# A graph network kernel on one core: loads, checks and scalings moved to other engines and slots

## The chip, the cores and the metric

The kernel runs on one core of one Trainium2 chip. The core has TensorE (matmuls; PE in the profile, PEld for its weight loads), VectorE (DVE), ScalarE (ACT), GpSimd (POOL) and SyncE (SP), each with a queue of its own that it works off in order. Sixteen DMA engines carry the transfers that SP, ACT and POOL issue. The metric is the device time of one execution in microseconds, as the median of several runs.

## What is computed

There are 16 graphs (B) of 1024 nodes (N) with 256 features (D). Each graph goes through two layers, and each layer ends with an addition and a norm over the features.

```python
# layer 0; adj holds 0 and 1 here, so only a0 counts
e0    = leaky(einsum('bid,bjd->bij', h * a0[:, 0], h))     # slope 0.2
alpha = sigmoid(where(adj == 1, e0, -huge))                # codes 2 to 4 use a1 to a3
x     = layernorm(x + einsum('bij,bjd->bid', alpha, h) + bias)
# layer 1
Hh = x @ W;  s = Hh @ a_src;  d = Hh @ a_dst
e  = where(adj != 0, exp(-leaky(s[:, None] + d[None, :])), 0)
x  = layernorm(x + elu((e @ Hh) / rowsum(e)))
```

Both norms are (x - mean) / sqrt(variance + 1e-5). The adjacency is symmetric and holds only 0 and 1; the kernel counts this while it runs, and a flag at the end decides whether a general version (`general_pass`) has to do the work again. With these inputs it does not.

## The kernel before

A graph passes through three stages, and TensorE goes through them one after the other. Nothing is scheduled by a tool inside `one_kind_pass`: the order of every engine's queue is the order in which the Python code emits the instructions (`manual_schedule`).

**Strips.** The score matrix is symmetric, so only the upper triangle is computed, in 8 strips of 128 rows (`strip(b, jt)`, L184 to L208). A strip has one or two pieces of up to 512 columns. For each piece TensorE multiplies x transposed (`xTs`) with x transposed and scaled by a0 (`xas`) into one of three PSUM banks (`ps_e`); ScalarE makes two tanh of it (`tb` at L206, `low` at L207, since a sigmoid is a tanh); VectorE takes their maximum (L208). `finish` (L214) adds one and multiplies by the adjacency, and POOL adds to the diagonal block (L224). The lower triangle is the mirror: for graph 0 TensorE transposes it (`mirror`, L252 and L253), for the others VectorE transposes blocks of 32 (`dump`, L230), SP writes them to DRAM (L234), `gather` (L238) reads them back and `mask` (L244) applies the adjacency. There are four `tb` buffers, so strip 4 and later wait until an earlier strip has been written out.

**First sum.** `sum0(b, t)` (L287 to L306) multiplies alpha with x for 128 rows, 8 tiles a graph. VectorE evicts each tile (L302) and takes mean and variance (`stats`, L264 and L265); after tiles 3 and 7 POOL works out one over the standard deviation (`rstd`, L267 to L280, six small operations). `scale0` then normalises a tile in place on VectorE (L283): x1.

**Second layer.** x1 has to be transposed for the projection: `save_x1` (L320) writes half a graph to DRAM, `fetch_x1` (`load_blocks`, L110, eight transfers) reads it back in blocks of 32, `turn_x1` (L331) transposes the blocks on VectorE. `project` (L343, and L351 to L353 on ScalarE) makes H and the two logits and stands between the strips of the next graph; `spread_p` (L362) spreads one logit along the rows. The second sum is `sum1` (L382) with `weights` (L375) as its factor; `elu` (L397 to L403) evicts a tile with three small operations on VectorE and a Relu and an Exp on ScalarE; `add` (L408, L409 and `stats`) finishes it on VectorE; the scaling of the second norm (`scale1`, L283, on VectorE) and the store (L432) come during the first sum of the graph two later.

So beside TensorE's stages of graph b, VectorE and ScalarE work on graphs b, b - 1 and b - 2. In the loop over b, `prev` is b - 1 and `done` is b - 2.

**Start and end.** x of graph 0 is transposed on TensorE (L179); x of the later graphs is loaded in blocks (`load_blocks`) and transposed on VectorE (`turn_x`, L169, and L170 on ScalarE). For graph 1 this load is issued by ScalarE's queue, for the others by SP's. `make_Wx` (L155 and L156) multiplies W with a, ahead of graph 0's first strip. `check_adj` (L116, ScalarE, 128x2048, four a graph, in the slots of tiles 4 to 7 of the first sum) counts the entries that are neither 0 nor 1. For graph 0 the strips 4 to 7 lie between the tiles of the first sum. For the last graph the scalings of the second norm are done on ScalarE (`scale1_act`, L425), with `center` (L412 to L420), which has POOL work out one over the deviation and minus the mean over the deviation.

Tiles of one tag share buffers: `a_bc` shares with p, graph 1's `xT` with y, and the check's `junk` with the products of `make_Wx`.

Of the kernel before, what the change touches and what calls it, by code (L numbers as in the profile page):

```python
# [9 lines left out]
F32 = mybir.dt.float32  # L10
# [3 lines left out]
AF = mybir.ActivationFunctionType  # L14
# [4 lines left out]
P = 128  # L19
# [10 lines left out]
def one_kind_pass(  # L30
# [70 lines left out]
                    continue  # L101
                nc.gpsimd.dma_start(adjs[b][v], rows[v])

    def load_blocks(dst, src, n0, n, queue=nc.sync):


        v = src[ds(n0, n), :].rearrange("(nb nn) (c q dd) -> q c nn nb dd", nn=SQ, c=ND, dd=SQ)
        for c in range(ND):
            for q in range(P // SQ):
                queue.dma_start(  # L110
                    dst[ts(q, SQ), c, ds(n0, n)].rearrange("p (nb dd) -> p nb dd", dd=SQ), v[q, c]
                )

# [28 lines left out]
    nc.gpsimd.memset(power, -0.5)  # L142
    bias_bc = const.tile([P, D], F32, tag="bias", name="bias_bc")
    nc.sync.dma_start(bias_bc, bias.partition_broadcast(P))
    a_bc = one.tile([P, 2 * D], F32, tag="p", name="a_bc")
    nc.sync.dma_start(a_bc, a[0].partition_broadcast(P))
    Wx = const.tile([P, ND, D + 2], F32, tag="Wx", name="Wx")
    nc.sync.dma_start(Wx[:, :, 2:], W.rearrange("(c p) o -> p c o", p=P))
# [130 lines left out]
        nc.gpsimd.tensor_tensor(r, r, n, ALU.mult)  # L279
        return r  # L280

    def scale(y, mv, r):
        nc.vector.tensor_scalar(y, y, mv[:, 0:1], r, ALU.subtract, ALU.mult)  # L283

    x1s, mv0s, r0s = {}, {}, {}

    def sum0(b, t):  # L287
        if t == 0:
            x1s[b] = two.tile([P, NT, D], F32, tag="x1", name=f"x1_{b}")
            mv0s[b] = small.tile([P, NT, 2], F32, tag="mv0", name=f"mv0_{b}")  # L290
            r0s[b] = {}
        acc = ps_acc.tile([P, D], F32, tag="acc", name=f"acc0_{b}_{t}")
        for jt in range(NT):
            nc.tensor.matmul(  # L294
                acc,
                lhsT=als[b][:, jt, ts(t, P)],
                rhs=xs[b][:, jt, :],
                start=(jt == 0),
                stop=(jt == NT - 1),
            )  # L300
        y = x1s[b][:, t, :]
        nc.vector.scalar_tensor_tensor(y, acc, 0.5, bias_bc, ALU.mult, ALU.add)  # L302
        stats(y, mv0s[b][:, t, :], f"0_{b}_{t}")
        if t % HT == HT - 1:
            g = t // HT
            r0s[b][g] = rstd(mv0s[b][:, ts(g, HT), :], f"0_{b}_{g}")  # L306

    def scale0(b, t):
        scale(x1s[b][:, t, :], mv0s[b][:, t, :], r0s[b][t // HT][:, t % HT : t % HT + 1])


    x1Ts, Hs, pqs, p_bcs, es = {}, {}, {}, {}, {}
# [16 lines left out]
    def turn_x1(b, g):  # L329
        v = x1Ts[b][:, :, ts(g, HALF)]  # L330
        nc.vector.transpose(v, v)  # L331
# [44 lines left out]
            es[b][:, m, :], p_bcs[b], pqs[b][:, m, 1:2], adjs[b][:, m, :], ALU.mult, ALU.min  # L376
        )

    hs, ys, mv1s, r1s, rms = {}, {}, {}, {}, {}

    def sum1(b, t, acc, m):
        nc.tensor.matmul(  # L382
# [29 lines left out]
    def center(b, t0, n):  # L412

        mv = mv1s[b][:, ds(t0, n), :]
        r = rstd(mv, f"1_{b}_{t0}")
        mr = small.tile([P, NT], F32, tag="mr", name=f"mr_{b}_{t0}")[:, 0:n]
        nc.gpsimd.tensor_tensor(mr, mv[:, :, 0], r, ALU.mult)
        nc.gpsimd.tensor_scalar(mr, mr, -1.0, None, ALU.mult)
        for t in range(n):
            rms[b, t0 + t] = r[:, t : t + 1], mr[:, t : t + 1]  # L420

    def scale1_act(b, t):
        y = ys[b][:, t, :]
        r, mr = rms[b, t]
        nc.scalar.activation(y, y, AF.Identity, bias=mr, scale=r)  # L425

    def scale1(b, t):
        scale(ys[b][:, t, :], mv1s[b][:, t, :], r1s[b][:, t : t + 1])

    def store(b, t0, n):  # L430
        rows = out[b].rearrange("(t p) d -> p t d", p=P)
# [7 lines left out]
    for g in range(2):  # L439
        for c in range(ND):  # L440
            transpose_x(0, g, c)
    make_Wx()
    strip(0, 0)
    for jt in range(HT):
        if jt < HT - 1:
            strip(0, jt + 1)
        finish(0, jt, 0, HALF)
        mirror(0, jt)
    load_x(1)
    new_xT(1)  # L450
    load_blocks(xTs[1], x[1], 0, N, nc.scalar)
    for t in range(NT):
        sum0(0, t)
        if t < HT:
            finish(0, t, HALF, N)
            strip(0, t + HT)
        if 1 <= t <= HT:
            finish(0, t + HT - 1)
            if t < HT:
                mirror(0, t + HT - 1)  # L460
        if t in (4, 5):
            scale0(0, 2 * t - 8)
            scale0(0, 2 * t - 7)
        if t == 5:
            save_x1(0, 0)
            fetch_x1(0, 0)
        if t in (5, 6):
            turn_x(1, t - 5)
        if t >= NT - CHECKS:
            check_adj(0, t - NT + CHECKS)  # L470

    for b in range(1, B):
        prev, done = b - 1, b - 2
        last = b == B - 1

        projects = [[jt] for jt in range(NT)]
        if prev == 0:

            projects = [[], [], [], [0, 1], [2, 3], [], [4, 5], [6, 7]]
        for jt in range(NT):  # L480
            strip(b, jt)
            if prev == 0 and jt in (1, 2):
                scale0(0, 2 * jt + 2)
                scale0(0, 2 * jt + 3)
            if prev == 0 and jt == 2:
                save_x1(0, 1)
                fetch_x1(0, 1)
            if prev == 0 and jt in (2, 5):
                turn_x1(0, (jt - 2) // 3)
            finish(b, jt)  # L490
            if jt < NT - 1:
                dump(b, jt)
            if jt >= 1:
                gather(b, jt - 1)
            for t in projects[jt]:
                project(prev, t)
            if jt >= 5:
                mask(b, jt - 5)
# [24 lines left out]
        if not last:  # L523
            load_adj(b + 1)


        for t in range(NT):
            acc = acc1(prev, t, ps_acc, "acc")
            for m in range(NT):
                sum1(prev, t, acc, m)  # L530
            if last and t == 6:
                turn_x1(b, 1)
            if last and t == 7:
                weights(b, 0)
                weights(b, 1)
            elu(prev, t, acc)
            if t >= 1:
                add(prev, t - 1)
            if t == 0:
                fetch_x1(b, 0)  # L540
            if t in (1, 2):
                scale0(b, 2 * t + 2)
                scale0(b, 2 * t + 3)
            if t == 2:
                save_x1(b, 1)
            if t == 4:
# [12 lines left out]


    last, done = B - 1, B - 2
    first = [acc1(last, t, ps_e, "e") for t in range(3)]
    for m in range(NT):
        if m >= 2:
            weights(last, m)
        if m == 3:
            add(done, NT - 1)
            center(done, 0, NT)
        for t in range(3):
            sum1(last, t, first[t], m)  # L570
    check_pq(last)
    for t in range(NT):
        if t < 3:
            acc = first[t]
        else:
            acc = acc1(last, t, ps_acc, "acc")
            for m in range(NT):
                sum1(last, t, acc, m)
        elu(last, t, acc)
        if t in (3, 6):  # L580
            center(last, t - 3, 3)
        add(last, t)
        if t == 6:
            center(last, 6, 1)
        for q in range(2 * t - 6, 2 * t - 4) if 3 <= t < 7 else []:
            scale1_act(done, q)
            if q in (3, 7):
                store(done, q - 3, HT)
        if t == 6:
            for q in range(3):  # L590
                scale1_act(last, q)
            store(last, 0, 3)
    for q in range(3, 7):
        scale1_act(last, q)
        if q == 5:
            store(last, 3, 3)
    center(last, 7, 1)
    scale1_act(last, 7)
    store(last, 6, 2)


# [389 lines left out]
```

## Time and profile before

| | us |
|---|---|
| median of 3 runs (lowest, highest) | 1329.43 (1328.62, 1329.67) |
| the profiled execution: time | 1330.3 |
| its span, first to last instruction | 1328.4 |
| TensorE busy | 1280.3 (96%) |
| VectorE busy | 1019.5 (77%) |
| ScalarE busy | 546.5 (41%) |
| POOL busy | 243.4 (18%) |
| one graph in the middle | 80.7 |
| mean granted TensorE clock | 0.992 |

The profile is of one execution, whose time stands beside its span. Times in it count from the span's start. A line of the timeline gives start, length, engine, code line, operation, written and read tile, shape and count; in brackets stand the idle time before it and what ended that. A wait is put down to what came last. Ends of matmuls are modelled, so neighbouring ones overlap by some 0.2 us. ACTq and SPq are the issue of transfers by that engine's queue.

### The profile page before, as it was taken

The page shows a single profiled execution, that of the slowest core. Times are in us where ns is not written, and L with a number is a line of the kernel's source. Part 1 is how long each engine was busy: PE and PEld are TensorE (multiplying, and loading weights), DVE is VectorE, ACT ScalarE, POOL GpSimd, SP SyncE. Part 2 cuts the span into 40 slices and gives each one's busy share as a digit, 9 for nine tenths or more (in the row PEclk, how much of TensorE's full clock was granted, in tenths as well). Part 3 has the DMA queues.
Part 4 walks back from the last instruction along what each step waited for, and adds up shares of the span by engine and source line. Part 5 has one row for each costly group of instructions (what it writes and reads, how often), then busy time and mean ns, then how long its engine had stood idle before and what let it go on. Part 6 is the DMA issues. An engine that isn't in the chain of part 4 may idle for free.

```text
span 1328.4 us, 17516 instructions
## 1 busy us (share of the span) xinstructions
PE 1280.3 (96%) x5550; PEld 1037.4 (78%) x5550; DVE 1019.5 (77%) x2318; ACT 546.5 (41%) x1236; POOL 243.4 (18%) x486
## 2 busy tenths in 40 slices
PE   7879999999999999999999999999999999999995
PEld 5758788687887878788687887878778687787874
DVE  5576886968869687886878869687886878869764
ACT  3352452715336162452715336162451624427034
POOL 2111111211112122111211112122111211112113
PEclk9999999999999999999999999999999999999998
DMA  9265687575677756687575677856686565775211
GB/s 215 54 133 113 109 174 143 113 164 104 145 141 157 160 103 150 109 180 143 111 162 106 150 138 152 162 105 151 111 177 130 110 151 106 172 143 111 68 29 66
DMA packets 606516, 173.36 MB, mean 130 GB/s; under 512 B 485584, under 2 KB 590928, under 8 KB 606416
## 3 DMA queue, kind: packets, MB, share of 16 engines
q1 hardware_dynamic: 580144, 137.56, 48.0%
q0 software_dynamic: 17952, 33.56, 14.8%
q10 hardware_dynamic: 8320, 1.05, 0.5%
q8 instruction: 46, 0.75, 0.2%
q14 instruction: 54, 0.44, 0.1%
HBM read 144.57 MB, written 61.08 MB: 155 GB/s over the span
## 4 chain that ended last, share of the span: by engine, by line
PE 83%; DVE 6%; DMA 3%; ACT 3%; SPq 2%; ACTq 1%; issue 1%; POOL 0%; DVEq 0%; POOLq 0%
PE acc L294 32%; PE acc L382 32%; PE pe L198 13%; PE pH L343 5%; DMA mir<-tb 2%; SPq L234 2%; DVE tb L208 1%; DVE al L214 1%; ACTq L110 1%; DVE tb L230 1%; ACT tb L206 1%; PE pp L362 1%; ACT low L207 1%; DVE st L264 1%; DVE y L409 0%
## 5 line engine op out<-in xcount | busy, mean ns | idle before, releaser
L382 PE MATMUL acc<-H,e 128*128 128x257 f32 x2048 | 448.7, 380 | 1.6 <-DVE e L375 1.6
L294 PE MATMUL acc<-x,al 128*128 128x256 f32 x2048 | 448.5, 381 | 0.0
L382 PEld LDWEIGHTS acc<-H,e 128*128 128x128 f32 x2048 | 387.9, 190 | 59.5 <-DVE e L375 2.4
L294 PEld LDWEIGHTS acc<-x,al 128*128 128x128 f32 x2048 | 389.5, 191 | 53.5 <-issue 0.5
L402 ACT ACTIVATE h<-acc,rinv 128x256 f32<-128x256 f32 x128 | 60.2, 470 | 562.2 <-DVE rinv L400 559.3
L198 PE MATMUL pe<-xa,xT 128*128 128x384 f32 (+3 forms) x768 | 269.4, 488 | 0.2 <-ACT low L207 0.2
L198 PEld LDWEIGHTS pe<-xa,xT 128*128 128x128 f32 x768 | 143.3, 191 | 87.5 <-issue 42.6
L271 POOL TENSOR_SCALAR ve<-mv 128x4 f32<-128x4 f32 (+3 forms) x51 | 18.0, 352 | 811.4 <-DVE mv L265 796.7
L375 DVE SCALAR_TENSOR_TENSOR e<-p,pq,adj 128x1024 f32<-128x1024 f32 x128 | 162.8, 1275 | 2.8 <-ACT p L363 2.8
L206 ACT ACTIVATE tb<-pe 128x512 f32<-128x512 f32 (+1 forms) x192 | 94.3, 491 | 136.5 <-PE pe L198 87.2
L343 PE MATMUL pH<-Wx,x1T 128*128 128x258 f32 x512 | 133.0, 386 | 7.1 <-DVE x1T L331 4.2
L343 PEld LDWEIGHTS pH<-Wx,x1T 128*128 128x128 f32 x512 | 97.2, 193 | 43.0 <-issue 17.6
L116 ACT ACTIVATE junk<-adj,minus 128x2048 bf16<-128x2048 bf16 x64 | 128.4, 2007 | 1.5
L397 DVE COPY rs<-acc 128x1 f32<-128x1 f32 x128 | 19.7, 154 | 138.9 <-PE acc L382 138.5
L208 DVE TENSOR_TENSOR tb<-tb,low 128x512 f32<-128x512 f32 (+1 forms) x192 | 99.3, 542 | 28.4 <-ACT low L207 25.8
L224 POOL TENSOR_TENSOR al<-ident,al 128x128 f32<-128x128 f32 x128 | 68.9, 538 | 240.9 <-DVE al L214 240.9
L214 DVE SCALAR_TENSOR_TENSOR al<-tb,adj 128x512 f32<-128x512 f32 (+7 forms) x132 | 99.4, 753 | 4.1
L302 DVE SCALAR_TENSOR_TENSOR x<-acc,bias_bc 128x256 f32<-128x256 f32 x128 | 54.3, 424 | 60.4 <-PE acc L294 59.2
L207 ACT ACTIVATE low<-pe 128x512 f32<-128x512 f32 (+1 forms) x192 | 93.3, 486 | 3.6 <-DVE tb L208 3.5
L273 POOL TENSOR_TENSOR r<-ve,power 128x4 f32<-128x4 f32 (+3 forms) x51 | 78.5, 1539 | 4.3
L230 DVE STREAM_TRANSPOSE tb<-tb 128x896 f32<-128x896 f32 (+6 forms) x105 | 74.7, 712 | 3.6
L244 DVE SCALAR_TENSOR_TENSOR al<-al,adj 128x896 f32<-128x896 f32 (+6 forms) x105 | 72.9, 694 | 0.9 <-DMA al<-mir 0.7
(58 smaller groups left out, 866.3 us busy)
## 6 DMA issues: line engine op xcount, KB each, us to landing
adj<-in_adjT POOLq DMA_DIRECT2D x30, 1024.0 KB, 13.6
x_rows<-x SPq DMA_DIRECT2D x32, 512.0 KB, 3.7
x1T<-x_rows SPq DMA_DIRECT2D x256, 64.0 KB, 2.4
x<-in_x SPq DMA_DIRECT2D x15, 1024.0 KB, 6.2
out<-y SPq DMA_DIRECT2D x30, 512.0 KB, 3.0
xT<-in_x SPq DMA_DIRECT2D x112, 128.0 KB, 3.2
mir<-tb SPq DMA_DIRECT2D x60, 112.0 KB, 2.4
al<-mir SPq DMA_DIRECT2D x15, 448.0 KB, 4.1
```

The source lines that it names most:

```text
L116: nc.scalar.activation(junk, adjs[b][:, ts(n, NT // CHECKS), :], AF.Square, bias=minus1, scale=2.0, accum_out=chk[:, b * CHECKS + n : b * ...
L198: nc.tensor.matmul(pe[:, 0:w], lhsT=xTs[b][:, c, ts(jt, P)], rhs=xas[b][:, c, ds(jt * P + o, w)], start=(c == 0), stop=(c == ND - 1),)
L206: nc.scalar.activation(tb[:, ds(o, w)], pe[:, 0:w], AF.Tanh, scale=0.5)
L207: nc.scalar.activation(low[:, 0:w], pe[:, 0:w], AF.Tanh, scale=0.5 * SLOPE)
L208: nc.vector.tensor_tensor(tb[:, ds(o, w)], tb[:, ds(o, w)], low[:, 0:w], ALU.max)
L214: nc.vector.scalar_tensor_tensor(als[b][:, jt, c0:c1], tbs[b, jt][:, c0 - jt * P : c1 - jt * P], 1.0, adjs[b][:, jt, c0:c1], ALU.add, ALU. ...
L230: nc.vector.transpose(tb, tb)
L273: nc.gpsimd.tensor_tensor(r, ve, power[:, 0:n_t], ALU.pow)
L294: nc.tensor.matmul(acc, lhsT=als[b][:, jt, ts(t, P)], rhs=xs[b][:, jt, :], start=(jt == 0), stop=(jt == NT - 1),)
L343: nc.tensor.matmul(pt, lhsT=x1Ts[b][:, c, ts(t, P)], rhs=Wx[:, c, :], start=(c == 0), stop=(c == ND - 1),)
L375: nc.vector.scalar_tensor_tensor(es[b][:, m, :], p_bcs[b], pqs[b][:, m, 1:2], adjs[b][:, m, :], ALU.mult, ALU.min)
L382: nc.tensor.matmul(acc, lhsT=es[b][:, m, ts(t, P)], rhs=Hs[b][:, m, :], start=(m == 0), stop=(m == NT - 1),)
```

## The change

- Graph 1's x is loaded by SP instead of ScalarE's queue. `a_bc` now shares its buffer with y, and so with graph 1's `xT`.
- `make_Wx` stands behind the first four strips of graph 0 instead of ahead of them.
- The checks of graph 0 stand in the slots of tiles 0 to 3 of the first sum (behind strips 4 to 7), those of the other graphs stay at tiles 4 to 7.
- Both norms are scaled on ScalarE (L292 of the new file) in all graphs, with factor and offset from `center` on POOL (two small operations more for each statistic, L287 and L288).
- In graph 1's strips the four scalings of x1's second half, its save and its fetch stand in strip 1, the transposes of x1 behind strips 3 and 6, and the projections behind strips 4, 5 and 7.
- In the last graph's second sum an addition stands behind the next tile's eviction; one of its weights is emitted a step earlier, and the addition and the statistics of the graph before two weights later.

```diff
-    a_bc = one.tile([P, 2 * D], F32, tag="p", name="a_bc")
+    a_bc = one.tile([P, 2 * D], F32, tag="y", name="a_bc")
...
-    def scale(y, mv, r):
-        nc.vector.tensor_scalar(y, y, mv[:, 0:1], r, ALU.subtract, ALU.mult)
+    def center(mv, what):
+        r = rstd(mv, what)
+        n = mv.shape[1]
+        mr = small.tile([P, NT], F32, tag="mr", name=f"mr_{what}")[:, 0:n]
+        nc.gpsimd.tensor_tensor(mr, mv[:, :, 0], r, ALU.mult)
+        nc.gpsimd.tensor_scalar(mr, mr, -1.0, None, ALU.mult)
+        return [(r[:, t : t + 1], mr[:, t : t + 1]) for t in range(n)]
+
+    def scale(y, r, mr):
+        nc.scalar.activation(y, y, AF.Identity, bias=mr, scale=r)
...
-    make_Wx()
     strip(0, 0)
     for jt in range(HT):
...
         mirror(0, jt)
+    make_Wx()
     load_x(1)
     new_xT(1)
-    load_blocks(xTs[1], x[1], 0, N, nc.scalar)
+    load_blocks(xTs[1], x[1], 0, N)
...
-        if t >= NT - CHECKS:
-            check_adj(0, t - NT + CHECKS)
+        if t < CHECKS:
+            check_adj(0, t)
...
-            projects = [[], [], [], [0, 1], [2, 3], [], [4, 5], [6, 7]]
+            projects = [[], [], [], [], [0, 1], [2, 3], [], [4, 5, 6, 7]]
         for jt in range(NT):
             strip(b, jt)
-            if prev == 0 and jt in (1, 2):
-                scale0(0, 2 * jt + 2)
-                scale0(0, 2 * jt + 3)
-            if prev == 0 and jt == 2:
+            if prev == 0 and jt == 1:
+                for t in range(HT, NT):
+                    scale0(0, t)
                 save_x1(0, 1)
-                fetch_x1(0, 1)
-            if prev == 0 and jt in (2, 5):
-                turn_x1(0, (jt - 2) // 3)
             finish(b, jt)
             if jt < NT - 1:
                 dump(b, jt)
+            if prev == 0 and jt == 1:
+                fetch_x1(0, 1)
+            if prev == 0 and jt in (3, 6):
+                turn_x1(0, (jt - 3) // 3)
             if jt >= 1:
                 gather(b, jt - 1)
...
             elu(prev, t, acc)
+            if last and t == 7:
+                weights(b, 2)
             if t >= 1:
                 add(prev, t - 1)
...
-            r1s[prev] = rstd(mv1s[prev], f"1_{prev}")
+            r1s[prev] = center(mv1s[prev], f"1_{prev}")
...
     for m in range(NT):
-        if m >= 2:
+        if m >= 3:
             weights(last, m)
-        if m == 3:
+        if m == 5:
             add(done, NT - 1)
-            center(done, 0, NT)
+            r1s[done] = center(mv1s[done], f"1_{done}")
...
         elu(last, t, acc)
+        if 1 <= t < NT - 1:
+            add(last, t - 1)
+        if t == 6:
+            add(last, t)
         if t in (3, 6):
-            center(last, t - 3, 3)
-        add(last, t)
+            r1s[last] += center(mv1s[last][:, ds(t - 3, 3), :], f"1_{last}_{t - 3}")
+        if t == 7:
+            add(last, t)
         if t == 6:
-            center(last, 6, 1)
+            r1s[last] += center(mv1s[last][:, 6:7, :], f"1_{last}_6")
```

More of the change, by code (lines that the diff above doesn't have):

```diff
@@ L102, in load_adj, with load_blocks @@
                 nc.gpsimd.dma_start(adjs[b][v], rows[v])
-    def load_blocks(dst, src, n0, n, queue=nc.sync):
+    def load_blocks(dst, src, n0, n):
         v = src[ds(n0, n), :].rearrange("(nb nn) (c q dd) -> q c nn nb dd", nn=SQ, c=ND, dd=SQ)
@@ L109, in load_blocks @@
             for q in range(P // SQ):
-                queue.dma_start(
+                nc.sync.dma_start(
                     dst[ts(q, SQ), c, ds(n0, n)].rearrange("p (nb dd) -> p nb dd", dd=SQ), v[q, c]
@@ L290, in sum0 @@
             mv0s[b] = small.tile([P, NT, 2], F32, tag="mv0", name=f"mv0_{b}")
-            r0s[b] = {}
+            r0s[b] = []
         acc = ps_acc.tile([P, D], F32, tag="acc", name=f"acc0_{b}_{t}")
@@ L305, in sum0 @@
             g = t // HT
-            r0s[b][g] = rstd(mv0s[b][:, ts(g, HT), :], f"0_{b}_{g}")
+            r0s[b] += center(mv0s[b][:, ts(g, HT), :], f"0_{b}_{g}")
     def scale0(b, t):
-        scale(x1s[b][:, t, :], mv0s[b][:, t, :], r0s[b][t // HT][:, t % HT : t % HT + 1])
+        scale(x1s[b][:, t, :], *r0s[b][t])
     x1Ts, Hs, pqs, p_bcs, es = {}, {}, {}, {}, {}
@@ L377, in weights @@
         )
-    hs, ys, mv1s, r1s, rms = {}, {}, {}, {}, {}
+    hs, ys, mv1s, r1s = {}, {}, {}, {}
     def sum1(b, t, acc, m):
@@ L410, in add @@
         stats(y, mv1s[b][:, t, :], f"1_{b}_{t}")
[L412 to L425, printed above, removed]
     def scale1(b, t):
-        scale(ys[b][:, t, :], mv1s[b][:, t, :], r1s[b][:, t : t + 1])
+        scale(ys[b][:, t, :], *r1s[b][t])
     def store(b, t0, n):
@@ L557, in one_kind_pass @@
             add(prev, NT - 1)
-            r1s[prev] = rstd(mv1s[prev], f"1_{prev}")
+            r1s[prev] = center(mv1s[prev], f"1_{prev}")
     last, done = B - 1, B - 2
+    r1s[last] = []
     first = [acc1(last, t, ps_e, "e") for t in range(3)]
     for m in range(NT):
-        if m >= 2:
+        if m >= 3:
             weights(last, m)
-        if m == 3:
+        if m == 5:
             add(done, NT - 1)
-            center(done, 0, NT)
+            r1s[done] = center(mv1s[done], f"1_{done}")
         for t in range(3):
@@ L579, in one_kind_pass @@
         elu(last, t, acc)
+        if 1 <= t < NT - 1:
+            add(last, t - 1)
+        if t == 6:
+            add(last, t)
         if t in (3, 6):
-            center(last, t - 3, 3)
-        add(last, t)
+            r1s[last] += center(mv1s[last][:, ds(t - 3, 3), :], f"1_{last}_{t - 3}")
+        if t == 7:
+            add(last, t)
         if t == 6:
-            center(last, 6, 1)
+            r1s[last] += center(mv1s[last][:, 6:7, :], f"1_{last}_6")
         for q in range(2 * t - 6, 2 * t - 4) if 3 <= t < 7 else []:
-            scale1_act(done, q)
+            scale1(done, q)
             if q in (3, 7):
@@ L590, in one_kind_pass @@
             for q in range(3):
-                scale1_act(last, q)
+                scale1(last, q)
             store(last, 0, 3)
     for q in range(3, 7):
-        scale1_act(last, q)
+        scale1(last, q)
         if q == 5:
             store(last, 3, 3)
-    center(last, 7, 1)
-    scale1_act(last, 7)
+    r1s[last] += center(mv1s[last][:, 7:8, :], f"1_{last}_7")
+    scale1(last, 7)
     store(last, 6, 2)
```

## The prediction

> **What bounds the kernel now.** I read the page's chain of waits first, then the windows of the span's start and end by microsecond, then the timelines of those stretches and of one graph in the middle (600 to 690 us).
>
> ```profile
> PE 83%; DVE 6%; DMA 3%; ACT 3%; SPq 2%; ACTq 1%; issue 1%; POOL 0%; DVEq 0%; POOLq 0%
> ```
>
> Most of the span is TensorE at work. A middle graph takes 80.7 us, and its only wait on TensorE is some 2 us at the end of the strips, for the last strip's tanh (behind the mirror transfers). What can be saved therefore lies in graph 0, in graph 1's strips and in the tail. Timeline of graph 0 (start, length, engine, line, operation; in brackets the idle time before and its releaser):
>
> ```profile
> 23.48 13.73 ACTq L110 DMA_DIRECT2D xT<-in_x  x7
> ...
> 34.29 1.45 PE L198 MATMUL pe<-xa,xT 128*128 128x384 f32 x4
> ...
> 37.32 0.60 ACT L206 ACTIVATE tb<-pe 128x512 f32<-128x512 f32 x1 [13.60 <-DMA xT<-in_x]
> ...
> 39.27 0.87 PE L252 MATMUL pal<-ident,tb 128*128 128x128 f32 x3 [3.54 <-DVE tb L208]
> ...
> 39.94 4.69 PE L294 MATMUL acc<-x,al 128*128 128x256 f32 x16
> ```
>
> ScalarE's queue issues graph 1's loads from 23.07 to 37.2; strip 4's tanh is queued behind them, and TensorE stands for the transposes of that strip. The next sum takes 4.69 where its neighbours of the same shape take 3.62: the granted clock was 0.50 from 39 to 42. In graph 1's strips:
>
> ```profile
> 63.57 5.31 PE L198 MATMUL pe<-xa,xT 128*128 128x512 f32 x12
> ...
> 63.85 1.99 ACT L116 ACTIVATE junk<-adj,minus 128x2048 bf16<-128x2048 bf16 x1
> ...
> 69.06 0.69 DVE L208 TENSOR_TENSOR tb<-tb,low 128x512 f32<-128x512 f32 x1 [4.19 <-ACT low L207]
> ...
> 79.66 3.68 PE L343 MATMUL pH<-Wx,x1T 128*128 128x258 f32 x8 [4.19 <-DVE x1T L331]
> ```
>
> Two checks (63.85 to 68.06) hold back the first tanh; VectorE starts on the strips 5.5 us after TensorE; TensorE pauses 4.19 us for the transposed x1, and its next eight matmuls take 3.68 instead of 1.91 at a clock of 0.50 (80 to 83). Graph 1's first sum starts at 97.4, 33.8 after its first strip; in a middle graph it is 25.4. The tail:
>
> ```profile
> 1314.13 0.25 POOL L271 TENSOR_SCALAR ve<-mv 128x3 f32<-128x3 f32 x1 [5.80 <-DVE rs L397]
> ...
> 1317.36 0.22 POOL L271 TENSOR_SCALAR ve<-mv 128x1 f32<-128x1 f32 x1
> ...
> 1320.29 0.22 POOL L271 TENSOR_SCALAR ve<-mv 128x1 f32<-128x1 f32 x1
> ...
> 1322.87 0.60 ACT L425 ACTIVATE y<-y,mr,r 128x256 f32<-128x256 f32 x1 [2.08 <-POOL mr L418]
> ```
>
> The last three statistics of the last graph follow one another on POOL, 3.2, 2.9 and 2.6 us. The end is set by when the first of them may start.
>
> **Loads of graph 1 on SyncE, checks early.** TensorE's work up to 35.7 is unchanged. Strip 4's products end at 31.0; the two tanh (0.49 + 0.59) and the maximum (0.69) end near 33, before TensorE comes to the transposes at 35.7. So the 3.54 us go, and with them the slow clock: 4.69 - 3.62 = 1.07, and some 0.3 of the 0.87. Gain 4.9. The checks now lie on ScalarE between the strips, 2.1 us each: 32.3 to 34.4 (strip 5's products end at 35.7), 37 to 39 (strip 6's at 40.4), 41.2 to 43.3 (strip 7's at 44.6), 45.1 to 47.2. Each fits a gap while TensorE sums, so they cost nothing. If a gap were gone a check would cost up to 2.1.
>
> SyncE's loads need the buffer of the W a product, moved behind the first half of the strips. Those four operations (0.76 + 0.69, twice: 2.9 us) run from 26.5 to 29.4, beside the first sum, whose eviction was at 29.3: 0 to 0.2, hidden, since TensorE has two more accumulators. Taking them from 12.7 to 15.7 gains at most 0.26 (one tanh's wait for VectorE), since the next steps wait for ScalarE anyway; taken as 0. Eight loads issued from 29 last between 4.0 (eight x1T loads in a middle graph) and 14.2 (these loads before, while the adjacency transfers run) and land 3 later: 36 to 46. They are read by VectorE's transpose, at 52.7 now. Nothing else stands in SyncE's queue until x1 is saved at 51. Cover 6 us, cost 0.
>
> [...]
>
> **Graph 1's strips.** Everything before them is 4.9 earlier: the first product at 58.7. The scalings of x1 on ScalarE (49 to 51) let SyncE save and fetch the first half by 60. Without checks VectorE's first maximum comes 3.1 after the first product (5.5 before): 61.8. From there VectorE needs for strips 0 to 3, by its rows less the four scalings, about 13 us, so that transposing x1's first half ends at 76.1 (79.6 before). TensorE's strips 2 to 4 run only as ScalarE frees its three banks, until 71.9. The pause is thus about 4.2 again, with the slow clock again (3.7 instead of 1.8 for two projections). Then strip 5 (1.3), two projections (1.7), strip 6 (0.9): 83.7. New is that the second half's transpose stands behind strip 6: tanh, maximum, mask, transpose (2.2), x1 transpose (1.25), four projections (3.5), last row and spread (0.8): the sum starts near 91.6 instead of 97.4. Gain 5.8 in all, 0.9 beyond the 4.9. ScalarE's four scalings (0.49 each, 2.0 us, behind strip 1) push strip 2's tanh to 68.4, where VectorE wants it at 69.8: hidden by 0.6, else up to 2.
>
> **Scalings on ScalarE in the middle.** 240 scalings leave VectorE (0.35 each as a pair takes 0.70) and go to ScalarE (five in 2.56: about 0.5 each). Per graph 16, of which 12 in the first sum, where ScalarE stood idle for 22.4 us, and 4 behind evictions of the second sum, each followed by a gap of 2.64 us. VectorE waits for TensorE in both sums, so its 5.6 us are no gain. POOL gets two operations per statistic (0.19 and 0.25, with gaps 0.55): the adjacency load is issued 0.55 later, with 23 us to its use, and the first diagonal addition 0.55 later, needed 16 us on. x1's second half is saved at 616.8 (616.9 before). Taken as 0 per graph; bounds -0.05 to +0.1, so -0.7 to +1.4 for 14 graphs.
>
> [...] If the scalings were on the path, 240 x 0.15 = 36 us would be lost; the rows show ScalarE idle there, and I go by them.
>
> **The tail.** The third weight now stands behind an eviction instead of before it: TensorE waits at other places, but VectorE's total to the last weight is the same, and TensorE ends within 0.1. An addition no longer follows its own exponential (0.99 of idle per tile), so VectorE keeps up with TensorE: tile 6 is ready at 1310.6, eviction (0.57) and addition 5 (1.47) end at 1312.7, and POOL's first statistic starts then instead of at 1314.1. Statistics of 3.2, 2.9 and 2.6 follow (their inputs come at 1314.1 and 1317.5, in time): 1.4 earlier. Bounds 0.9 to 2.
>
> **Sum.** 4.9 + 0.9 + 0 + 1.4 = 7.2. The profiled execution has a span of 1328.4 and a time of 1330.3, so a span of 1321.2 and a time of 1323.1; the median of the runs shown, 1329.43, stands 0.9 lower: 1322.2.
>
> **Rivals.** One: the pause in graph 1's strips falls under what slows the clock (pauses of 2.72 left it at 1.00, of 4.2 did not; mine is worked out to within a microsecond). Then 1.9 more: 1320.3. For it: VectorE has four scalings less. Against: TensorE's stretch before the pause ends earlier too.
>
> Two: SyncE's queue. The fetch of x1's second half now stands before the first gather and waits for the save to land: 4.6 us here before, 7.9 in a middle graph under the adjacency load. With 7.9, gather, masks and the dump that strip 6 needs come 3.3 later, and a pause of over 4 before the last projections brings the slow clock again: 1325 to 1327.
>
> Three, slower: ScalarE is late with the second half of x1 in every graph. That half's fetch was issued until 628.8 and lands about 2.4 later; VectorE's transpose, first in the chain that sets the strips' length, reads it at 633.9. Beyond 2.6 us of lateness each microsecond is paid in 14 graphs; 0.5 beyond cancels the gain, 1 beyond gives 1336. Against it: the gaps of 2.64 behind the evictions.
>
> **Chances.** Within 0.2% (2.7 us) is about what a measurement of this kernel can't tell from no change. Forecast 0.58; clock kept 0.18; SyncE's queue 0.14, a third of it within 0.2%; ScalarE late 0.08, most of it slower; 0.02 for no effect at all. Faster 0.85, same 0.09, slower 0.06. Range: 1318.5 (the clock kept, with the bounds of tail and middle) to 1326.5 (the second rival's middle and a little).
>
> **What would show it.** Right: no wait on TensorE between 30 and 58 and a clock of 1.00 there; the first strip of graph 1 at 58.7; its first sum near 91.6; 80.7 us per graph; the last scaling at 1322.9 - 7.2 = 1315.7. Wrong: a transpose of graph 1's x waiting for its load; a graph of over 81 us; a first sum of graph 1 later than 94.

## The result, and the profile after

The changed kernel takes 1322.81 us (median of 7 runs, 1320.53 to 1325.36) against 1329.43 (7 runs, 1328.28 to 1332.45): a ratio of 0.995, 95% interval 0.9936 to 0.9965. The prediction was 1322.2, in a range from 1318.5 to 1326.5. The profiled execution has a span of 1321.0 and a time of 1322.8. It and the profiled execution of before (1330.3) are 7.5 apart, the medians 6.6; the stretches below are those of the two profiled executions.

Five starting points that every trace here shows end five stretches of the span: graph 0's first sum, graph 1's first strip product, graph 1's first sum, graph 15's first sum, and the last scaling.

| stretch, us | before | predicted change | after | change |
|---|---|---|---|---|
| A: start to graph 0's first sum | 25.66 | 0 | 24.24 | -1.42 |
| B: to graph 1's first product | 37.91 | -4.9 | 32.80 | -5.11 |
| C: graph 1's strips, to its first sum | 33.65 | -0.9 | 35.87 | +2.22 |
| D: 14 graphs, to graph 15's first sum | 1122.58 | 0 | 1120.33 | -2.25 |
| E: to the last scaling | 103.07 | -1.4 | 102.07 | -1.00 |
| sum | | -7.2 | | -7.56 |

The sum came out; of its five terms only B and, roughly, E did. The prediction read graph 1's first sum of before at 97.4; the trace has 97.22 (63.57 + 33.65), so by its own 91.6 the term of C should have been 0.7 and not 0.9. First the timeline of after, from the start into graph 0's first sum:

```profile
10.76 0.60 ACT L206 ACTIVATE tb<-pe 128x512 f32<-128x512 f32 x1 [0.30 <-PE pe L198]
...
24.24 3.62 PE L303 MATMUL acc<-x,al 128*128 128x256 f32 x16
27.35 9.93 SPq L110 DMA_DIRECT2D xT<-in_x  x8
...
29.72 0.60 ACT L206 ACTIVATE tb<-pe 128x512 f32<-128x512 f32 x1 [7.42 <-DVE al L214]
30.69 2.00 ACT L116 ACTIVATE junk<-adj,minus 128x2048 bf16<-128x2048 bf16 x1
...
34.16 0.49 PE L252 MATMUL pal<-ident,tb 128*128 128x128 f32 x3
34.49 3.62 PE L303 MATMUL acc<-x,al 128*128 128x256 f32 x16
```

SyncE now issues the loads; strip 4's tanh comes at 29.72 instead of 37.32, the check follows in the gap, the transposes wait for nothing and the next sum takes 3.62 instead of 4.69. The start is A's. In before the first products are longer, and the W a product (`wprod`) follows the first tanh:

```profile
8.89 7.85 PE L198 MATMUL pe<-xa,xT 128*128 128x512 f32 x16
...
12.05 0.60 ACT L206 ACTIVATE tb<-pe 128x512 f32<-128x512 f32 x1 [1.51 <-PE pe L198]
...
12.72 0.76 DVE L155 TENSOR_TENSOR wprod<-Wx,a_bc 128x256 f32<-128x256 f32 x2 [2.90 <-DMA Wx<-in_W]
```

In after the same sixteen matmuls start at 8.84 and take 6.61. Graph 1's strips of after:

```profile
57.04 13.12 PE L198 MATMUL pe<-xa,xT 128*128 128x512 f32 x36
...
60.07 0.69 DVE L208 TENSOR_TENSOR tb<-tb,low 128x512 f32<-128x512 f32 x1 [1.73 <-ACT low L207]
...
73.21 1.20 DVE L340 STREAM_TRANSPOSE x1T<-x1T 128x1024 f32<-128x1024 f32 x1
...
74.47 3.81 PE L352 MATMUL pH<-Wx,x1T 128*128 128x258 f32 x8 [4.31 <-DVE x1T L340]
...
78.07 2.66 PE L198 MATMUL pe<-xa,xT 128*128 128x384 f32 x4
...
81.67 0.56 DVE L208 TENSOR_TENSOR tb<-tb,low 128x384 f32<-128x384 f32 x1 [5.35 <-ACT low L207]
...
86.79 5.41 PE L352 MATMUL pH<-Wx,x1T 128*128 128x258 f32 x16 [3.00 <-issue]
...
92.91 2.32 PE L303 MATMUL acc<-x,al 128*128 128x256 f32 x10
```

Up to 74.4 all is as predicted: VectorE starts 3.0 after the first product, x1's transpose ends 17.4 after it, the pause is 4.31. A projection is four matmuls (some expectations below count the matmuls under that name). The first two projections (x8: 3.81, at full clock 1.91), strip 5 (2.66, in graph 0 1.45) and the last four projections (x16: 5.41, in e8 3.76) are slow. The windows of the same trace (length, then PE, PEld, DVE, ACT and POOL busy, the granted clock, and the DMA engines' busy share and GB/s) show the clock falling:

```profile
70.00:72.00 2.00, 0.16 (x1) 0.00 (x0) 1.93 (x5) 1.19 (x2) 0.45 (x1) 1.00 1.26 196
72.00:74.00 2.00, 0.00 (x0) 0.00 (x0) 1.97 (x3) 0.00 (x0) 0.45 (x1) 0.92 0.68 108
74.00:76.00 2.00, 1.53 (x4) 1.25 (x5) 1.93 (x4) 0.00 (x0) 0.21 (x1) 0.50 0.83 131
```

In windows of 0.2 us it is 0.50 from 73.7 to 80.5 and from 87.3 to 90.7. The tail, with the three statistics again 3.2, 2.8 and 2.6 apart:

```profile
1306.72 0.32 POOL L271 TENSOR_SCALAR ve<-mv 128x3 f32<-128x3 f32 x1 [6.79 <-DVE mv L265]
...
1309.92 0.23 POOL L271 TENSOR_SCALAR ve<-mv 128x1 f32<-128x1 f32 x1
...
1312.73 0.22 POOL L271 TENSOR_SCALAR ve<-mv 128x1 f32<-128x1 f32 x1
1315.31 0.60 ACT L292 ACTIVATE y<-y,mr,r 128x256 f32<-128x256 f32 x1 [2.02 <-POOL mr L288]
```

### The profile page after: what moved, and what is told of

Its sections match the earlier page's. It is cut to its first block, busy times and chain, and to the rows that moved or that the text cites. A ratio compares the mean times of both kernels' runs of the same rounds, so it can differ in the third digit from the quotient of the medians.

```text
span 1321.0 us, 17670 instructions
## 1 busy us (share of the span) xinstructions
PE 1279.7 (97%) x5550; PEld 1038.1 (79%) x5550; DVE 940.9 (71%) x2078; ACT 661.5 (50%) x1476; POOL 289.1 (22%) x578
## 5 line engine op out<-in xcount | busy, mean ns | idle before, releaser
L292 ACT ACTIVATE x<-x,mr,r 128x256 f32<-128x256 f32 x128 | 69.2, 592 | 217.6 <-POOL mr L288 217.6
L224 POOL TENSOR_TENSOR al<-ident,al 128x128 f32<-128x128 f32 x128 | 64.6, 509 | 209.8 <-DVE al L214 209.8
## 6 DMA issues: line engine op xcount, KB each, us to landing
adj<-in_adjT POOLq DMA_DIRECT2D x30, 1024.0 KB, 13.5
```

## The experiments

All stretches in one table, from each kernel's profiled execution, with its ratio to the kernel before on the same chip. "First tanh" is the first on graph 0's strips; "half clock in C" is the time at a granted clock of 0.50 within that stretch (twice what the clock lacked of 1.00).

| kernel | first tanh | A | B | C | half clock in C | D | E | ratio (95%) |
|---|---|---|---|---|---|---|---|---|
| before | 12.05 | 25.66 | 37.91 | 33.65 | 3.4 | 1122.58 | 103.07 | |
| after | 10.76 | 24.24 | 32.80 | 35.87 | 6.8 + 3.4 | 1120.33 | 102.07 | 0.995 (0.9936-0.9965) |
| e1_loads | 11.31 | 24.80 | 32.79 | 33.82 | 3.4 | 1123.99 | 103.08 | 0.9957 (0.9943-0.9971) |
| e2_early | 11.13 | 25.60 | 32.80 | 33.72 | 3.4 | 1122.24 | 103.05 | 0.998 (0.9968-0.9992) |
| e3_scalings | 10.65 | 25.60 | 38.16 | 35.21 | 6.8 | 1120.82 | 103.70 | 1.0009 (0.9998-1.0021) |
| e4_tail | 11.84 | 25.60 | 39.41 | 33.90 | 6.8 | 1127.15 | 101.50 | 0.999 (0.9977-1.0004) |
| e5_order | 11.94 | 25.42 | 32.79 | 33.04 | 3.4 + 3.4 | 1125.18 | 102.07 | 0.9936 (0.9911-0.9961) |
| e6_fill | 11.78 | 25.26 | 32.79 | 32.90 | 3.4 | 1121.37 | 102.06 | 0.9922 (0.9899-0.9945) |
| e7_late | 11.26 | 24.75 | 32.79 | 30.44 | 3.4 | 1124.21 | 102.07 | 0.9898 (0.9872-0.9923) |
| e8_turns | 10.83 | 24.31 | 32.79 | 32.04 | 5.1 | 1122.32 | 102.07 | 0.9903 (0.988-0.9927) |
| after_again | 11.41 | 24.90 | 32.79 | 35.69 | 3.4 + 6.8 | 1121.83 | 102.07 | 0.9942 (0.9929-0.9956) |
| e9_gpsimd | 11.83 | 25.32 | 32.79 | 32.38 | 6.8 | 1126.10 | 101.47 | 0.9922 (0.9908-0.9936) |
| e10_checks | 11.78 | 25.26 | 32.80 | 34.28 | 3.4 + 3.4 | 1126.58 | 101.51 | 0.9944 (0.9929-0.9958) |
| e11_joined | 11.99 | 25.48 | 32.79 | 31.62 | 3.4 | 1122.47 | 101.52 | 0.9912 (0.9893-0.9932) |

**The loads with their place (e1).** The kernel before with:

```diff
-    make_Wx()
     strip(0, 0)
...
+    make_Wx()
     load_x(1)
     new_xT(1)
-    load_blocks(xTs[1], x[1], 0, N, nc.scalar)
+    load_blocks(xTs[1], x[1], 0, N)
```

and `a_bc` in tag "y". 

> The kernel before with three edits of the change: the loads of graph 1's x issued by SyncE, the W a product moved behind the first four strips, its buffer taken from the tag of those loads. Checks, scalings, graph 1's order and the tail stay as before. Theory (the prediction's first term): no wait behind strip 4, the clock at 1.00 from 30 to 58 us, graph 1's first product 4.9 earlier than 63.57, its first sum 4.9 earlier than 97.4, and 4.9 us less in all: about 1324.5. Rival (who issues a load hardly matters): under 1 us. Rival on the start: in the trace of after the first sum began 1.42 earlier (24.24 for 25.66). If the W a product's place does that, it begins near 24.2 here too, and the gain is 6.3; if it was the slow first products of the run before (0.86 us each from 8.9 to 11.8, 0.43 in after), it begins anywhere from 24.2 to 25.4, by how this run's clock starts.

B falls from 37.91 to 32.79, and by nothing else than these edits: 5.1. All kernels with SyncE's loads show 32.79 or 32.80; the three with ScalarE's show 37.91, 38.16 and 39.41, and the longest of them, e4's, has 6.8 us of half clock from 38 us on where the others have 3.4. The time falls by 0.43% (0.29 to 0.57), 3.9 to 7.6 us. A is 24.80, between the two readings of the start, 13.49 behind the first tanh: see below.

**The loads alone (e2).** The kernel before with `nc.scalar` taken out of that one call. 

> The kernel before with one edit: the same eight loads issued by SyncE, everything else in place, so nothing holds them back and SyncE issues them from about 5 us, while graph 0's adjacency (needed by VectorE's first mask at 18.2) is under way. Theory: the 1 MB shares the DMA engines with the adjacency, whose share is already over 1.1 there, and at some 250 GB/s the first masks and the first sum come up to 4.2 us later; the 4.9 of the loads remains, so 0.7 to 4.9 less than before: 1324.5 to 1328.7. Rival (time of issue is all that counts): 1324.5, first sum at 25.7 as before. The W a product stands in front here: if it costs time only when the first products run at full speed, the fourth strip piece's second tanh is seen waiting for VectorE until about 16.3 whatever the start.

```profile
4.42 32.45 SPq L110 DMA_DIRECT2D xT<-in_x  x8
...
58.40 5.31 PE L198 MATMUL pe<-xa,xT 128*128 128x512 f32 x12
```

The issue begins at 4.42 and stretches over 32 us beside graph 0's adjacency, and costs nothing: A is 25.60, graph 1's first product 5.17 earlier. The theory that the early loads would delay the first masks falls. The timed gain, 0.2% (0.08 to 0.32, so 1.1 to 4.3 us), is smaller than the 5.1 of the profiled execution. That one, with 1325.22, was the fastest of the twelve (median 1327.74), which may be a part of the difference; the rest stays open.

**Scalings alone (e3).** Both norms on ScalarE, with the two more operations on POOL, every call in its old place:

```diff
-        nc.vector.tensor_scalar(y, y, mv[:, 0:1], r, ALU.subtract, ALU.mult)
+        nc.scalar.activation(y, y, AF.Identity, bias=mr, scale=r)
```

> The kernel before with the scalings of both norms moved from VectorE to ScalarE (with the two more statistics operations on GpSimd), all in their old places; nothing else. Theory (the prediction's zero): from graph 1's first sum to the last eviction of graph 14's sums 1186.9 us as before, within 1; in graph 1's strips ScalarE's four scalings push the tanh by up to 2 us; in all 0 to +2: 1329.4 to 1331.4. Rival: VectorE's 5.6 us less per graph are worth 0.1 us per graph, which would explain the 1.5 us that the middle of after gained beyond the prediction: 1328. Rival two (ScalarE late with x1): 1 us or more per graph, over 1340.

The time is 1.0009 of before (0.9998 to 1.0021): -0.3 to +2.8 us. C is 35.21, 1.6 more than in before, with 6.8 us of half clock for 3.4. D is 1120.82 here; over all kernels it is 1122.2 to 1127.2 with the scalings on VectorE and 1120.3 to 1126.6 on ScalarE. Split into TensorE's pauses (those over 0.15 us) and the rest, it tells why. The rest is 1106.5 to 1106.6 where the loop has no half clock (e2, e3, e6; 1107.4 in e8, whose stretch in C runs 1.7 us into D), 1108.1 to 1108.3 in the seven kernels with one stretch, 1109.8 with two (e9) and 1111.6 to 1111.8 with three (e4, e10): 1.7 for each, half of its 3.4. The pauses make 12.2 to 17.0. Before and after have one stretch each, and 2.1 of the 2.25 that D lost in after lie in the pauses (12.24 for 14.35). The same kernel again has 13.51, the other eight with the scalings on ScalarE have 14.2 to 17.0, and the four with them on VectorE 14.4 to 15.8: nothing shown gives the 2.25 to the scalings. What the scalings do cost is 0.6 in E: 103.70. VectorE's first operation on all checks (`bad`, written behind everything in the code) stands in VectorE's queue within graph 15's first sum. In before, with ScalarE's last check done at 1229.4:

```profile
1229.40 0.20 DVE L941 TENSOR_SCALAR bad<-chk 128x64 f32<-128x64 f32 x1 [1.59 <-ACT junk L116]
```

and in after, where scalings that wait for POOL stand ahead of the checks on ScalarE:

```profile
1242.45 0.20 DVE L943 TENSOR_SCALAR bad<-chk 128x64 f32<-128x64 f32 x1 [4.40 <-ACT junk L116]
...
1243.11 1.25 DVE L384 SCALAR_TENSOR_TENSOR e<-p,pq,adj 128x1024 f32<-128x1024 f32 x1
...
1244.42 1.79 PE L391 MATMUL acc<-H,e 128*128 128x257 f32 x7 [0.34 <-DVE e L384]
```

VectorE stands 4.40 us, graph 14's last weight comes late, and TensorE waits for it.

This trace also settles the start. Its first products ran at full speed early (first tanh at 10.65), and yet:

```profile
10.65 0.60 ACT L206 ACTIVATE tb<-pe 128x512 f32<-128x512 f32 x1 [0.19 <-PE pe L198]
...
12.66 0.76 DVE L155 TENSOR_TENSOR wprod<-Wx,a_bc 128x256 f32<-128x256 f32 x2 [2.92 <-DMA Wx<-in_W]
...
15.57 2.67 DVE L208 TENSOR_TENSOR tb<-tb,low 128x512 f32<-128x512 f32 x4
16.29 0.60 ACT L207 ACTIVATE low<-pe 128x512 f32<-128x512 f32 x1 [1.61 <-DVE tb L208]
```

VectorE holds the W a product, which waits for W until 12.66; the first maximum comes at 15.57, and the third piece's second tanh, which needs one of two `low` buffers, comes at 16.29. In the four kernels with the product in front, A is 25.60 to 25.66, wherever the first tanh is between 10.65 and 12.05. In the ten with it behind, A is the first tanh plus 13.48 or 13.49. So the move gains 25.6 - 13.5 - (first tanh): 1.4 in after, 0.1 with e11's start at 11.99.

**Tail alone (e4).** Weight 2, the additions and graph 14's norm in their new slots. 

> The kernel before with the tail's edits alone (third weight behind the last eviction of graph 14, additions of the last graph behind the next eviction, graph 14's norm two weights later). Theory: the first of the last three statistics on GpSimd starts 1.4 us earlier counted from the eviction of graph 14's last tile, and so does the last scaling: 1328.0. Rival (the moved weight holds TensorE back as much as the additions gain): 0, 1329.4.

E is 101.50: 1.57 less. The theory holds in the trace; in time (0.9977 to 1.0004) it can't be told from nothing. With the 0.6 of the scalings this makes after's 102.07.

**Graph 1's old order (e5).** The changed kernel with the old placing of scalings, save, fetch, transposes and projections. 

> The changed kernel with graph 1's strips in the old order: scalings, save and fetch of x1's second half behind strips 1 and 2, its transposes behind strips 2 and 5, projections behind strips 3, 4, 6 and 7. Theory: the new order is what made graph 1's strips 35.9 us from first product to first sum, 3.0 more than predicted; with the old order and without checks in front of the tanh the stage takes 31.4 to 33.8 and the first sum starts between 88.5 and 91 (92.9 in after), 2 to 4 us less in all. Rival: both orders end alike, since SyncE's queue (dumps and fetch) sets the stage: 92.9, no difference.

C is 33.04, 2.8 less than in after and inside the range given (the first sum, at 91.25, just above its own), so in these traces the new order is the longer one. This one too has half clock twice, after pauses of 1.86 and 3.97, but 6.8 us of it in all where after has 10.2. With 6.8 the new order takes 34.28 (e10): of the 2.8 that is 1.6 for the clock and 1.2 for the order. In time (0.9911 to 0.9961) it isn't told apart from after.

**The pauses filled (e6).** The changed kernel with:

```diff
+            if prev == 0 and jt in (4, 7):
+                fill = ps_t.tile([P, HT, P], F32, tag="t", name=f"fill_{jt}")
+                for n in range(16 if jt == 4 else 8):
+                    nc.tensor.transpose(fill[:, n % HT, :], ident2, ident)
             for t in projects[jt]:
```

> The changed kernel with TensorE given work of no use in its two pauses in graph 1's strips: 16 transposes of the identity behind strip 4's product, 8 behind strip 7's, into a PSUM buffer that nobody reads. Theory: the clock of 0.50 from 74 to 80 and 88 to 90 comes from the pauses of 4.31 and 3.00 us; with about 2.1 us and 1.1 us of each filled the clock stays at 1.00, eight projections take 1.9 instead of 3.81, strip 5 1.45 instead of 2.66, the last sixteen 3.5 instead of 5.41, and the first sum starts 3 to 5 us earlier: 88 to 90, and the time is 3 to 5 us less. Rival (the clock falls there for another reason, or VectorE's chain hides it): the slow stretches stay or the first sum still starts at 92.9.

```profile
71.01 1.91 PE L492 MATMUL fill<-ident,ident 128*128 128x128 f32 x16
...
75.48 3.55 PE L352 MATMUL pH<-Wx,x1T 128*128 128x258 f32 x8 [2.56 <-DVE x1T L340]
78.82 1.64 PE L198 MATMUL pe<-xa,xT 128*128 128x384 f32 x4
...
83.35 1.04 PE L492 MATMUL fill<-ident,ident 128*128 128x128 f32 x8
...
86.52 3.73 PE L352 MATMUL pH<-Wx,x1T 128*128 128x258 f32 x16 [2.13 <-DMA mir<-tb]
```

Half right: the second slow stretch is gone (3.73 for the last four projections instead of 5.41) and the first is halved, from 75.8 to 79.2, though the clock fell after a pause of only 2.56. C is 32.90, what the prediction had said for it (91.6 - 58.7 = 32.9), 3.0 less than in after; the first sum, at 90.95, misses the range because A is 1.0 later here. So the clock is what C lost against the prediction. The change's own order agrees: its C is 35.87 and 35.69 with 10.2 us of half clock, 34.28 with 6.8 (e10, which edits nothing there) and 32.90 here with 3.4.

**Strip 5 ahead of the projections (e7).** 

> The changed kernel with the first four projections of graph 0 behind strip 5 instead of behind strips 4 and 5, and the second transpose of x1 behind strip 5 instead of 6. Theory: VectorE's idle 5.35 us before strip 5's maximum came from strip 5's products standing behind four projections on TensorE; here strip 5's products run before the pause, VectorE goes on without it, and the first sum starts at 86 to 89 although the pause of 3 to 4 us and the slow clock after it stay: 4 to 7 us less than after. Rival (SyncE's queue of dumps, or the landing of x1's second half near 77.6, holds VectorE instead): 90 to 93.

```diff
-            projects = [[], [], [], [], [0, 1], [2, 3], [], [4, 5, 6, 7]]
+            projects = [[], [], [], [], [], [0, 1, 2, 3], [], [4, 5, 6, 7]]
...
-            if prev == 0 and jt in (3, 6):
-                turn_x1(0, (jt - 3) // 3)
+            if prev == 0 and jt in (3, 5):
+                turn_x1(0, (jt - 3) // 2)
```

```profile
74.96 5.26 PE L352 MATMUL pH<-Wx,x1T 128*128 128x258 f32 x16 [3.02 <-DVE x1T L340]
...
76.74 0.52 DVE L208 TENSOR_TENSOR tb<-tb,low 128x384 f32<-128x384 f32 x1
...
87.98 2.32 PE L303 MATMUL acc<-x,al 128*128 128x256 f32 x10
```

Not four projections, as the expectation has it, but two stand in front of strip 5 in after (x8 at 74.47). VectorE takes strip 5's maximum straight behind strip 4 (76.74), with no wait of 5.35; C is 30.44, the shortest here, with the pause of 3.02 and 3.4 us of half clock still in it. The first sum starts at 87.98, as expected. In time the ratio is 0.9898 (0.9872 to 0.9923), below both intervals of after. Those are from other series, on other chips, each against the kernel before in the same one; so far as they compare, this version beats after as well as before.

**Transposes earlier (e8).** Transposes of x1 behind strips 2 and 4, projections behind 4 and 7. 

> The changed kernel with x1's two transposes on VectorE behind strips 2 and 4 (3 and 6 in the change) and the projections four at a time behind strips 4 and 7. Theory: x1's first half has landed by 61, so its transpose may come a strip earlier; TensorE's first pause is then under 2.7 us and the clock stays at 1.00; the second transpose starts as its half lands near 77.6; the first sum starts at 84 to 87, 6 to 9 us less than after. Rival: strip 5, now behind all four projections, comes late for VectorE, or the second half has not landed: first sum at 88 to 92.

```profile
72.15 3.76 PE L352 MATMUL pH<-Wx,x1T 128*128 128x258 f32 x16 [1.93 <-DVE x1T L340]
...
81.30 0.38 ACT L206 ACTIVATE tb<-pe 128x256 f32<-128x256 f32 x1 [3.19 <-PE pH L352]
...
84.48 0.28 ACT L206 ACTIVATE tb<-pe 128x128 f32<-128x128 f32 x1 [2.53 <-DMA mir<-tb]
...
85.55 2.09 PE L352 MATMUL pH<-Wx,x1T 128*128 128x258 f32 x4 [4.33 <-ACT H L360]
```

The first pause is 1.93, the clock stays at 1.00, and four projections take 3.76. Then the tanh of strips 6 and 7 wait for `tb` buffers that the dumps of strips 2 and 3 still read (for strip 6 the profile names a projection, whose result the tanh does not read; the last part of strip 2's dump landed at 81.19), the evictions of the last projections are queued behind them on ScalarE, and TensorE pauses 4.33. First sum at 89.14: the rival.

**The kernel again, and GpSimd's queue (after_again, e9, e10).** 

> The changed kernel itself, on the chip of the next two, so that they stand beside it. Theory: the first step to graph 0's first sum follows the moment at which the first products reach full speed (first tanh at 10.6 to 12.1) with 13.48 between; from the first sum to graph 1's first product 32.8; graph 1's stage 33 to 36 by how many of its pauses lower the clock; from graph 15's first sum to the last scaling 102.07. In all 5 to 8 less than before. Rival (the 35.87 of graph 1's stage and the early start are fixed): the same positions as before within 0.2.

A, B, C and E come as expected; 0.9942 (0.9929 to 0.9956) confirms the result. C is 35.69 with the half clock spread otherwise, 3.4 after the first pause and 6.8 after the second.

e9 is e8 with `fetch_x1(0, 1, nc.gpsimd)` and graph 15's checks in the first slots. 

> The changed kernel with x1's transposes behind strips 2 and 4 and the projections four at a time (as in the run with the earlier transposes), the fetch of x1's second half issued by GpSimd instead of SyncE, and graph 15's checks in the first four slots. Theory: in the run with the earlier transposes strips 6 and 7 waited for the buffers that the dumps of strips 2 and 3 read (3.19 and 2.53 us of idle time on ScalarE), and those dumps stood in SyncE's queue behind 4.25 us of fetch; without it both tanh come on time, graph 1's first sum starts at 83.5 to 86 (stage 26.4 to 29), and the tail is 0.6 shorter: 7 to 10 us less than the changed kernel. Rival: GpSimd issues more slowly, or its queue waits for the saved rows, x1's second half lands later than 77 and the first sum starts at 88 or later: under 4 us less.

```profile
71.89 5.27 POOL L110 DMA_DIRECT2D x1T<-x_rows  x8 [3.17 <-DMA x_rows<-x]
...
81.62 1.25 DVE L340 STREAM_TRANSPOSE x1T<-x1T 128x1024 f32<-128x1024 f32 x1 [4.04 <-DMA x1T<-x_rows]
```

Strip 6's tanh no longer waits (0.16), but the half lands at 81.6, 4.5 behind the end of its issue, which now runs beside the dumps (in e8 1.7 behind SyncE's). First sum at 90.49: the rival again.

e10 has those checks alone:

```diff
-            if t >= NT - CHECKS:
-                check_adj(b, t - NT + CHECKS)
+            n = t if last else t - NT + CHECKS
+            if 0 <= n < CHECKS:
+                check_adj(b, n)
```

> The changed kernel with graph 15's four checks in the first slots of its first sum instead of the last four; nothing else. Theory: with ScalarE's scalings in front of the last checks VectorE's operation on all checks (line 943) waits 4.40 us, the last weight of graph 14 behind it comes late, and TensorE stands 0.34 us: 0.6 us of the tail (103.7 for 103.07 where only the scalings were moved). Here that wait goes: from graph 15's first sum to the last scaling 101.45 instead of 102.07. Rival (the 0.6 comes from the scalings' own place): 102.07. In time 0.6 is less than the runs can tell.

```profile
1230.05 0.20 DVE L944 TENSOR_SCALAR bad<-chk 128x64 f32<-128x64 f32 x1 [1.27 <-ACT junk L116]
```

E is 101.51 for 102.07, and `bad` waits 1.27 instead of 4.40. The mechanism is shown; in time it is too small to see.

**Joined (e11).** e7 with e10's checks and 22 transposes of the identity in the pause. 

> The changed kernel with what the runs so far point to: projections of the first four tiles behind strip 5, x1's second transpose behind strip 5, graph 15's checks in the first slots, and 22 transposes of the identity (0.12 us each) on TensorE behind strip 5's product, in the pause of 3.0 us before those projections. Theory: the pause left is 0.4 us, the clock stays at 1.00 there, the sixteen projections take 3.7 instead of 5.26, graph 1's first sum starts 28.7 after its first product (30.44 with the slow clock, 35.87 in the change), and the tail takes 101.5: about 7.5 us less than the changed kernel with the profile of the record. Rival (ScalarE's evictions and the dumps set the end of the stage, not TensorE): the stage stays at 30.4 although the clock is 1.00.

```profile
75.70 3.76 PE L352 MATMUL pH<-Wx,x1T 128*128 128x258 f32 x16 [0.62 <-DVE x1T L340]
...
86.48 2.09 PE L352 MATMUL pH<-Wx,x1T 128*128 128x258 f32 x4 [3.08 <-ACT H L360]
```

The clock stays at 1.00 there and the four projections take 3.76, yet the first sum is not earlier: C is 31.62. What TensorE gains it waits off again before the last projections, whose buffers ScalarE empties only behind strip 7's tanh, and that longer pause brings the half clock back. The rival holds, as far as the waits show: past e7 the end of C is set by the dumps in SyncE's queue and by ScalarE's order. No run changes those alone. 0.9912 (0.9893 to 0.9932) is no better than e7.

## Why the prediction was right, and where not

**Loads: right.** 4.9 predicted, 5.1 measured in B, by the mechanism named (ScalarE's queue, then the clock). In e2 nothing but the issuing engine of eight loads changes, and B falls by 5.1; on SyncE, with nothing behind them, 32 us of issue cost nothing. On ScalarE's queue the issue took 14.1 us (23.07 to 37.2), and with ScalarE's work behind it it cost 5.1.

**Checks: right.** They lie in the gaps, and B is 32.79 with checks there (e5) and without (e1).

**W a product: the step failed.** "Taking them from 12.7 to 15.7 gains at most 0.26" was read from a trace in which the first products ran at half speed until 11.4 and so hid the product. The move gains 0.1 to 1.4, depending on when TensorE reaches full speed; 1.4 in the profiled execution of after.

**Graph 1's strips: the step failed.** The chain to 76.1 was right to 0.1 (17.37 for 17.4), the pause too ("about 4.2 again, with the slow clock again"). Mis-sized was the slow clock: it was charged to two projections only. It lasted 6.8 us, took strip 5 too (2.66 for 1.3), and came a second time after the pause before the last projections (5.41 for 3.5): +1.3 + 1.9 = 3.2, against 3.1 between the predicted 32.8 and the measured 35.9. e6, with 3.4 of those 10.2 us left, gives 32.90. The first rival ("clock kept") erred the other way; the second came near in its effect (a late second half, slow clock again), but not by its cause: VectorE stood 5.35 us for strip 5's product, which stood on TensorE behind the pause and two slow projections, as e7 shows. SyncE's queue becomes the limit only after that, by the waits of e8 and e11.

**Middle: 0 stands.** e3's interval of -0.3 to +2.8 us leaves no room for the third rival, a late ScalarE in every graph. D's -2.25 is scatter of TensorE's pauses. The prediction's 80.7 us for a graph was that of one graph; the mean over D is 80.18 in before and 80.02 in after.

**Tail: mechanism right, one term missed.** 1.57 by e4 for the 1.4 predicted; the 0.6 that the scalings cost through `bad` was not seen, since the operation that waits is written at the end of the code and stands in the middle of VectorE's queue.

That the sum came out is luck: in the two profiled executions +3.1 (strips) and +0.4 (tail) met -1.4 (start), -0.2 (loads) and -2.25 (loop).

## What to carry to other kernels

Before a step that seems hidden is priced at nothing, ask whether its cover is itself an accident of that execution: the W a product lay under a slow start that other executions don't have. A pause of TensorE costs its length and, after some of 1.86 to 3.02 us here and after all of 3.08 to 4.96 (below), 3.4 us of half clock or twice that, so short pauses are worth reordering for: a strip's products ahead of projections that must wait anyway made that stretch 3.2 us shorter than in before (e7), where the change made it 2.2 longer. When work is moved onto an engine, look in the trace for every instruction that waits for what now stands behind it, also for those that the code writes elsewhere.

## What the runs showed of the hardware

- Until the last matmuls the half clock came in stretches of 3.4 us (e6: 75.8 to 79.2; e7: 74.6 to 78.1; e5: 72.4 to 75.8) or 6.8 (after: 73.7 to 80.5; e8: 84.1 to 90.9). The length of the pause alone doesn't decide: after 3.02 us the clock fell in e7 and stayed at 1.00 in e3; after 1.86 it fell in e5, after 1.93 it stayed in e8. After the longer pauses seen from 30 us on, 3.08 (e11) to 4.96 (e3), it always fell.
- Within one trace too the shorter pause can be the one with the half clock: in e10 the clock was 0.50 from 254 to 256 after a pause of 1.90 us (TensorE's next matmul at 253.04) and 1.00 from 1058 to 1070 around one of 2.47 (1059.63). What else decides is not shown: no run moves a pause alone.
- At the start products of graph 0 followed one another every 0.85 us until 11.4 in before, and every 0.43 from the first one on in after, while the granted clock in the windows of both is 1.00 from 8 to 12: that row did not show the slow start, the matmuls did. The first tanh lies between 10.65 and 12.05 over these executions, which alone moves the kernels with the W a product behind by up to 1.3 us. What sets that moment is not shown.
- Eight block loads took SyncE 9.9 us to issue in after (27.35), 32.5 when started at 4.42, and 4.3 in graph 1's strips; GpSimd took 5.27 for eight, and from the end of the issue to VectorE's use of them it was 2.7 longer than with SyncE's (e9 against e8), beside the dumps.
